# Scores three tiles at a time, statistics turned in the sums' bank, and pieces at new places, in an attention and FFN block

## The chip, the core and the metric

The kernel runs on one core of a Trainium2 chip. The core has a matrix engine (TensorE, PE in the profile; its weight loads are PEld), a vector engine (DVE), a scalar engine for functions such as exp (ACT), a general engine (POOL), and a queue engine that issues most of the DMA transfers (SP). Each engine executes its own instructions in program order and waits for others by semaphores. PE writes its results to PSUM, a memory of eight banks of 512 floats for each of 128 partitions; DVE and ACT read them there, POOL does not.

The metric is the time of one execution on the device, in microseconds (us). Before the change it is 1064.85 us, the median of three runs (1061.61, 1064.85 and 1066.0).

## What is computed

The input `x` is 16 batches of 512 rows of 128 numbers. With `xn`, the normalised rows of `x`, the result is `x + attention(xn) + ffn(xn)`. In short:

```
q, k, v = xn @ Wq, xn @ Wk, xn @ Wv          # 16 heads; 8 numbers a head for q, k; 64 for v
scores  = q . k / sqrt(8), causal
ctx     = softmax(scores) @ v                # per head, over 512 keys
attn    = concat(ctx) @ Wo
xr, xk  = mixes of xn with the row before it, by mu_r and mu_k
ffn     = sigmoid(xr @ W_r.T) * (square(relu(xk @ W_k.T)) @ W_v.T)
out     = x + attn + ffn
```

Everything is float32.

## The kernel before

**Units and slots.** The heads go by pairs: two heads sit in partitions 0 to 63 and 64 to 127 of the same tile, so that PE computes both at once. Two pairs make a group `g`, four groups a batch `b`. The causal half of a group's scores is cut into blocks of 128 rows (or keys), and these are packed into five units, `u` = 0 to 4, each of which fills a PSUM tile of two banks (512 columns for each of the two heads). `ROW_UNITS` and `KEY_UNITS` (lines 31 to 44) list what each unit holds. There are 20 units in a batch and 320 in all. The main loop (line 612) goes through *slots*, one for each unit; a batch is 20 slots.

**Scores are computed twice.** First by rows: `row_scores` writes a tile `sm` with queries along the partitions, and `row_max` lets DVE take the maximum over each row (one instruction for each block and head, `CUSTOM_DVE_ANT` in the profile, followed by a short read of its accumulator). When a group's maxima are complete, `turn_stats` transposes them on PE into a tile `pm`, DVE splits them into a high and a low part (`mh`, `ml`), and SP copies these into rows of `q`, where they take part in the second computation. Then by keys: `key_scores` writes a tile `sT` with keys along the partitions, from which the maximum is already subtracted; ACT takes the exponential (`weights`, tile `e`), POOL zeroes what lies above the diagonal (`mask_weights`) and adds up the blocks of a pair (`add_weights`, tile `acc`). The rows run eight slots (`LEAD`) ahead of the keys.

**From weights to output.** `sum_weights` sums the weights over the keys on PE with a matrix of ones (tile `z`), and ACT takes the logarithm (`half`); `invert_sums` makes reciprocals of it with two more instructions on ACT and copies each to the other heads' partitions by SP (`recip`). Five slots (`LAG`) after the keys, `weigh` multiplies the weights with `v` on PE, into a tile `av` of one bank for each pair; `take_ctx` lets DVE multiply `av` by `recip` into `ctx`. `project_out` multiplies a group's two `ctx` with `Wo` (tile `po`) and DVE adds that to the FFN's result. `store` transposes the sum back (`yT`), DVE adds `x`, and SP stores it.

**Pieces.** The rest is cut into pieces that are placed at slots by the calls of `at` (lines 518 to 553): the eight products of `project_v` (tile `pv`, read by ACT), `project_qk` (tiles `pq` and `pk`; ACT takes the high part, DVE then the low part, SP writes both to DRAM and `spread_qk` brings them back), `transpose_xn`, the three products of the FFN (`ffn_k`, `ffn_r`, `ffn_out`), the moments and the layernorm of a later batch. Each has a slot and a place in it: -1 ahead of the scores, 0 and 1 after them, 2 at the slot's end.

**What sets the order.** `slot_work` (lines 559 to 595) writes the instructions down, and `_InOrder` keeps each engine's own in that order. In each slot: `turn_stats` where due, the pieces of place -1, `row_scores` and `key_scores`, in the slots with `u` = 4 the first pair's sums, then what ACT, POOL and DVE do with the scores, the pieces of places 0 and 1, `weigh`, in the slots with `u` = 1 the second pair's sums, `take_ctx` in those with `u` = 1 (first pair) and `u` = 4 (second pair), and the pieces of place 2.

**PSUM.** All eight banks are in use (lines 95 to 97): three buffers of two banks for the score tiles (`ps_sc`, which also gives the tile `pm`), one bank for `av`, and one bank, `ps_m`, for all other products in turn (`m_tile`: the sums `z`, `pv`, `pq`, `pk`, `po`, the FFN's, the transposes). A tile's next user waits until the last reader of the one before is done.

**Two ways of using PE.** `product`, `weigh` and `sum_weights` use four columns of 32 at a time, with all 128 rows of the array. The scores use 33 or 35 rows and 128 columns, for two heads at a time.

Of the kernel before, what the change touches and what calls it, by code (L numbers as in the profile page):

```python
# [9 lines left out]
FP = mybir.dt.float32  # L10
# [5 lines left out]
P = 128  # L16
# [6 lines left out]
UNITS = 5  # L23
LEAD = 8
LAG = 5
# [37 lines left out]
def attn_ffn_kernel(  # L63
# [19 lines left out]
    N_UNITS = B * PER_BATCH  # L83
# [11 lines left out]
    ps_sc = ctx.enter_context(tc.tile_pool(name="ps_sc", bufs=3, space=PSUM))  # L95
# [14 lines left out]
    def m_tile(name):  # L110
        return ps_m.tile([P, 512], FP, tag="m", name=name)
# [204 lines left out]
    def row_scores(n):  # L316
        b, g, u = place(n)
        q, k = qs[b % 2], ks[b % 2]
        sm = sms[n] = ps_sc.tile([P, 2, 512], FP, tag="sc", name=f"sm_{n}")
        for pair, i, at_col in ROW_UNITS[u]:  # L320
            p = 2 * g + pair
            for h in range(2):
                s = slice(64 * h, 64 * h + RS)
                pe.matmul(
                    sm[:, h, at_col : at_col + (i + 1) * P],
                    q[s, p, i * P : (i + 1) * P], k[s, p, : (i + 1) * P],
                    start=True, stop=True,
                )
# [13 lines left out]
                    accum_out=stats[b, g][:, h, pair, i : i + 1],  # L342
                )

    def turn_stats(b, g):
        mx = stats.pop((b, g))
        pm = ps_sc.tile([P, 2, 512], FP, tag="sc", name=f"pm_{b}_{g}")[:, 0]
        pe.transpose(pm[0 : 4 * NB, 0:P], mx.rearrange("q h p i -> q (h p i)"), ident)
        hi = stat.tile([4 * NB, P], FR, tag="mh", name=f"mh_{b}_{g}")
        lo = stat.tile([4 * NB, P], FR, tag="ml", name=f"ml_{b}_{g}")  # L350
        dve.tensor_copy(hi, pm[0 : 4 * NB, 0:P])
        dve.tensor_tensor(lo, pm[0 : 4 * NB, 0:P], hi.bitcast(FP), ALU.subtract)
        for n, half in enumerate((hi, lo)):
            for h in range(2):
                r = 64 * h + RS + n
                sp.dma_start(
                    out=qs[b % 2].bitcast(FP)[r : r + 1, 2 * g : 2 * g + 2, :].rearrange(
                        "o p (i t) -> o (p i) t", t=P
                    ),
                    in_=half.bitcast(FP)[2 * NB * h : 2 * NB * h + 2 * NB],  # L360
                )
# [5 lines left out]
    def place(n):  # L367
        b, r = divmod(n, PER_BATCH)
        return (b, *divmod(r, UNITS))

    def key_scores(n):
        b, g, u = place(n)
        q, k = qs[b % 2], ks[b % 2]
        st = sts[n] = ps_sc.tile([P, 2, 512], FP, tag="sc", name=f"sT_{n}")
        for pair, j, at_col in KEY_UNITS[u]:
            p, w = 2 * g + pair, T - j * P
            for h in range(2):
                s = slice(64 * h, 64 * h + RA)
                pe.matmul(
                    st[:, h, at_col : at_col + w],  # L380
                    k[s, p, j * P : (j + 1) * P], q[s, p, j * P : T],
                    start=True, stop=True,
                )

    def weights(n):
        e = es[n] = ep.tile([P, 2, 512], FP, tag="e", name=f"e_{n}")
        act.activation(e, sts.pop(n), AF.Exp)

    def mask_weights(n):

        e, parts = es[n], KEY_UNITS[n % UNITS]
        if n % UNITS == 2:
            blocks = [e.rearrange("k h (s q) -> k (h s) q", q=256)[:, :, 0:P]]
        else:
            blocks = [e[:, :, at_col : at_col + P] for _, _, at_col in parts]
        for d in blocks:
            pool.affine_select(
                out=d, in_=d, compare_op=ALU.is_ge, fill=0.0, base=0,
                pattern=[[0, d.shape[1]], [1, P]], channel_multiplier=-1,
            )  # L400
# [29 lines left out]
                acc[:, :, P:256], es[n][:, :, P:256], es[n - 1][:, :, 0:P], ALU.add  # L430
            )

    def sum_weights(q0, pair):


        e0, acc = es[q0 + 4 * pair], accs.pop((q0, pair))
        z = m_tile(f"z_{q0}_{pair}")
        for part in range(2):
            for c in range(2):
                if part and c:  # L440
                    continue
                lo, hi = ((0, P), (256, T))[c] if part == 0 else (P, 256)
                for h in range(2):
                    r = 64 * c + 32 * h
                    pe.matmul(
                        z[r : r + 32, lo - 256 * c : hi - 256 * c], ones[:, 0:32],
                        (acc if lo else e0)[:, h, lo:hi],
                        start=True, stop=True, skip_group_check=True,
                    )
        half = small.tile([P, 256], FP, tag="half", name=f"half_{q0}_{pair}")  # L450
        act.activation(half, z[:, 0:256], AF.Ln)
        recips[q0, pair] = half
# [57 lines left out]

    todo = {}

    def at(slot, where, f, *args):
        todo.setdefault((slot, where), []).append((f, args))

    for b in range(-1, B):
        s0 = b * PER_BATCH
        n = b + 2  # L520
        if n < B:
            first = n == 1
            for c in range(NB):
                at(c - 7 if first else s0 + 1 + c, 0, row_moments, n, c)
            at(-4 if first else s0 + 5, 0, layernorm, n)
            at(-3 if first else s0 + 6, 0, scale_xn, n)
            at(-3 if first else s0 + 8, 2 if first else 1, transpose_xn, n)
            at(-2 if first else s0 + 10, 2 if first else -1, project_qk, n, False)
            at(-1 if first else s0 + 15, 2 if first else -1, project_qk, n, True)
            for i in range(4):  # L530
                at(i if first else s0 + 20 + i, 0, spread_qk, n, False, i)
                at(i + 4 if first else s0 + 24 + i, 0, spread_qk, n, True, i)
        if b + 1 < B:
            places = ((5, -1), (8, 2), (12, 1), (13, 1), (13, 2), (17, 1), (23, 1), (23, 2))
            if b < 0:
                places = ((-8, 1), (-7, 1), (-6, 1), (-5, 1), (-4, 1), (-3, 1), (-1, 1), (3, 1))
            for n, (slot, where) in enumerate(places):
                at(slot + max(s0, 0), where, project_v, b + 1, n)
        if b < 0:
            at(-6, 2, turn_weights)  # L540
            continue
        if b + 3 < B:
            at(s0 + 12, 0, load_x, b + 3)
        at(s0 - 5, 0, mix, b, 1)
        at(s0 - 3, 0, mix, b, 0)
        at(s0 - 2, 1, ffn_k, b)
        at(s0, -1, ffn_r, b)
        at(s0, 0, ffn_log, b)
        at(s0 + 1, 0, ffn_sig, b)
        at(s0 + 2, 1, ffn_out, b)  # L550
        for g in range(NQ):
            at(s0 + 5 * g + 10, 2, project_out, b, g)
        at(s0 + 27, 1, store, b)

    def run(s, where):
        for f, args in todo.pop((s, where), ()):
            f(*args)

    def slot_work(s):
        rows = s + LEAD if s + LEAD < N_UNITS else None  # L560
        keys = s if 0 <= s < N_UNITS else None
        av = s - LAG if 0 <= s - LAG < N_UNITS else None
        u = s % UNITS
        turned = s + LEAD - UNITS
        if turned >= 0 and turned % UNITS == 0 and turned < N_UNITS:
            b, g, _ = place(turned)
            turn_stats(b, g)
        run(s, -1)
        if rows is not None:
            row_scores(rows)  # L570
        if keys is not None:
            key_scores(keys)
        first_sums = u == 4 and 0 <= s - 4 < N_UNITS
        if first_sums:
            sum_weights(s - 4, 0)
        if keys is not None:
            weights(keys)
            mask_weights(keys)
            add_weights(keys)
        if first_sums:  # L580
            invert_sums(s - 4, 0)
        if rows is not None:
            row_max(rows)
        run(s, 0)
        run(s, 1)
        if av is not None:
            weigh(av, only=1 if u == 2 else None)
            if u == 1:
                sum_weights(s - 6, 1)
                invert_sums(s - 6, 1)  # L590
                weigh(av + 1, only=0)
                take_ctx(av - 1, 0)
            if u == 4:
                take_ctx(av - 4, 1)
        run(s, 2)
# [13 lines left out]
    load_weights()  # L609
    for b in range(1, min(B, 3)):  # L610
        load_x(b)
    for s in range(-LEAD, N_UNITS + LAG):
        slot_work(s)
    for s, where in sorted(todo):
        run(s, where)
# [31 lines left out]
```

## Time and profile before

| | |
|---|---|
| median of three runs | 1064.85 us |
| the profiled execution, its own time | 1067.56 us |
| its span in the profile | 1065.8 us |
| PE busy | 965.3 us, 91% of the span |
| DVE busy | 790.7 us, 74% |
| POOL busy | 771.8 us, 72% |
| ACT busy | 669.1 us, 63% |
| chain that ended last: PE, ACT, DVE, POOL | 41%, 24%, 14%, 11% |
| row maxima on DVE: 1024 instructions | 508.4 us, mean 497 ns |
| reads of their accumulators: 1024 | 143.7 us, mean 140 ns |
| exponential of a key tile on ACT: 320 | 326.8 us, mean 1021 ns |
| a copy of `pv` on ACT: 128 | 76.2 us, mean 595 ns |
| logarithm of the sums on ACT: 128 | 49.0 us, mean 383 ns |
| reciprocals on ACT: 256 | 106.3 us, mean 415 ns |
| add of `po` on DVE: 64 | 44.1 us, mean 689 ns |

The span goes from the first instruction to the last of one profiled execution; the execution's own time has what lies around it too. An engine is busy while an instruction of it is under way, whether or not anything depends on it. Matmuls overlap each other, so for PE the distance from one start to the next says more than the length of one. A line of the timeline gives the start and the length in us, the engine, the line of the source, the instruction, what it writes and reads, the shape, how many were merged, and in brackets the idle time before it with what ended that. All kernel instructions carry line 57, that of the helper which records them, so they are told apart by their tiles. The granted clock of TensorE is 1.0 at full speed.

### The profile page before, as it was taken

The page shows a single profiled execution, that of the slowest core. Times are in us where ns is not written, and L with a number is a line of the kernel's source. Part 1 is how long each engine was busy: PE and PEld are TensorE (multiplying, and loading weights), DVE is VectorE, ACT ScalarE, POOL GpSimd, SP SyncE. Part 2 cuts the span into 40 slices and gives each one's busy share as a digit, 9 for nine tenths or more (in the row PEclk, how much of TensorE's full clock was granted, in tenths as well). Part 3 has the DMA queues.
Part 4 walks back from the last instruction along what each step waited for, and adds up shares of the span by engine and source line. Part 5 has one row for each costly group of instructions (what it writes and reads, how often), then busy time and mean ns, then how long its engine had stood idle before and what let it go on. Part 6 is the DMA issues. An engine that isn't in the chain of part 4 may idle for free.

```text
span 1065.8 us, 28371 instructions
## 1 busy us (share of the span) xinstructions
PE 965.3 (91%) x10563; PEld 417.8 (39%) x10563; DVE 790.7 (74%) x2628; ACT 669.1 (63%) x1041; POOL 771.8 (72%) x996
## 2 busy tenths in 40 slices
PE   1679999999999999999999999999999999999996
PEld 0123444344444434444443444344444444444442
DVE  1547787787878778787877788787778878778752
ACT  1235766757576666757676675767667676766752
POOL 3126877877787787878778787877778787778883
PEclk9957999999999999999999999999999999999999
DMA  5644254353626334362544436263443635352011
GB/s 122 107 80 82 52 92 96 62 95 73 102 64 98 89 70 86 72 106 69 91 90 76 78 72 106 69 94 87 76 80 79 98 80 87 72 83 46 20 35 26
DMA packets 61450, 84.25 MB, mean 79 GB/s; under 512 B 12208, under 2 KB 48688, under 8 KB 59264
## 3 DMA queue, kind: packets, MB, share of 16 engines
q1 hardware_dynamic: 58624, 80.79, 41.3%
q8 instruction: 84, 1.38, 0.6%
q0 software_dynamic: 448, 0.26, 0.4%
q10 hardware_dynamic: 2240, 1.38, 0.4%
q14 instruction: 54, 0.44, 0.2%
HBM read 39.13 MB, written 25.17 MB: 60 GB/s over the span
## 4 chain that ended last, share of the span: by engine, by line
PE 41%; ACT 24%; DVE 14%; POOL 11%; issue 6%; DMA 3%; SPq 0%; ACTq 0%; DVEq 0%; POOLq 0%
PE av L57 10%; ACT e L57 9%; PE po L57 8%; POOL acc L57 8%; PE pv L57 6%; PE z L57 5%; DVE sm L57 5%; ACT recip L57 4%; PE sm L57 4%; POOL e L57 3%; ACT e_sig L57 3%; PE sT L57 2%; ACT v L57 2%; PE pk L57 2%; DVE ffn L57 2%
## 5 line engine op out<-in xcount | busy, mean ns | idle before, releaser
L57 DVE CUSTOM_DVE_ANT_0 sm<-sm,row_mask 128x384 f32<-128x384 f32 (+3 forms) x1024 | 508.4, 497 | 136.8 <-PE sm L57 111.5
L57 ACT ACTIVATE e<-sT 128x1024 f32<-128x1024 f32 x320 | 326.8, 1021 | 150.3 <-PE sT L57 140.1
L57 PE MATMUL av<-e,v 128*32 128x512 f32 (+3 forms) x4096 | 353.1, 438 | 2.8 <-DVE ctx L57 2.7
L57 POOL TENSOR_SCALAR_AFFINE_SELECT e<-e 128x256 f32<-128x256 f32 (+1 forms) x448 | 197.0, 454 | 198.1 <-ACT e L57 193.9
L57 POOL TENSOR_TENSOR acc<-acc,e 128x256 f32<-128x256 f32 (+1 forms) x256 | 257.8, 1007 | 15.4
L57 POOL TENSOR_TENSOR acc<-e,e 128x768 f32<-128x768 f32 (+2 forms) x192 | 245.8, 1280 | 0.0
L57 PE MATMUL sm<-k,q 33*128 33x384 f32 (+3 forms) x1024 | 165.1, 379 | 20.1 <-DMA k<-kd 19.2
L57 PEld LDWEIGHTS av<-e,v 128*32 128x32 f32 x4096 | 127.3, 109 | 138.0 <-issue 106.2
L57 PEld LDWEIGHTS sm<-k,q 33*128 33x128 f32 x1024 | 83.5, 189 | 214.9 <-issue 112.2
L57 PE MATMUL pv<-wv,xnT 128*32 128x512 f32 x1024 | 143.3, 631 | 6.0 <-DVE ffn L57 4.4
L57 DVE DVE_READ_ACCUMULATOR2_ANT mx<- 128x1 f32 x1024 | 143.7, 140 | 0.0
L57 PE MATMUL sT<-q,k 35*128 35x384 f32 (+3 forms) x1024 | 137.3, 325 | 1.5 <-DVE mx L57 0.7
L57 ACT ACTIVATE v<-pv 128x512 f32<-128x512 f32 x128 | 76.2, 595 | 86.5 <-PE pv L57 71.8
L57 PE MATMUL po<-ctx,wo 128*32 128x512 f32 x1024 | 122.5, 595 | 7.6 <-DVE ql L57 3.2
L57 ACT ACTIVATE half<-z 128x256 f32<-128x256 f32 x128 | 49.0, 383 | 101.6 <-PE z L57 101.6
L57 DVE TENSOR_TENSOR ctx<-av,recip 128x512 f32<-128x512 f32 x128 | 87.7, 685 | 30.8 <-PE av L57 22.9
L57 ACT ACTIVATE recip<-half 64x256 f32<-64x256 f32 x256 | 106.3, 415 | 6.3
L57 PEld LDWEIGHTS sT<-q,k 35*128 35x128 f32 x1024 | 93.3, 189 | 11.6 <-issue 2.5
L57 PE MATMUL z<-acc,ones 128*32 128x256 f32 (+1 forms) x1024 | 79.4, 331 | 1.8 <-POOL acc L57 1.8
L57 POOL TENSOR_TENSOR xmix<-xmix,prev 128x512 f32<-128x512 f32 x32 | 41.0, 1281 | 43.9 <-ACT prev L57 43.9
L57 PEld LDWEIGHTS po<-ctx,wo 128*32 128x32 f32 x1024 | 30.2, 109 | 93.3 <-issue 47.6
L57 PE MATMUL z<-e,ones 128*32 128x128 f32 x512 | 51.9, 278 | 10.5 <-DVE ffn L57 4.1
(73 smaller groups left out, 632.6 us busy)
## 6 DMA issues: line engine op xcount, KB each, us to landing
recip<-recip SPq DMA_DIRECT2D x256, 64.0 KB
q<-qd SPq DMA_DIRECT2D x60, 256.0 KB
k<-kd SPq DMA_DIRECT2D x60, 256.0 KB
kd<-kh SPq DMA_DIRECT2D x64, 128.0 KB
x<-in_L_attn_x_dram SPq DMA_DIRECT2D x16, 256.0 KB
qd<-qh SPq DMA_DIRECT2D x32, 128.0 KB
qd<-ql SPq DMA_DIRECT2D x32, 128.0 KB
kd<-kl SPq DMA_DIRECT2D x32, 128.0 KB
```

The lines of the kernel that those rows point to most:

```text
L57: return self._tc.keep_in_program_order(f(*args, **kwargs))
```

## The change

The loop of slots is written anew. Scores are no longer computed in each slot, but twice in three slots, three tiles at a time: in slots `s` that are a multiple of 3 a row tile (unit `s + 8`), a key tile (`s`) and a row tile (`s + 9`); in the slot after it, behind the sums and the pieces of place 1, a key tile (`s`), a row tile (`s + 9`) and a key tile (`s + 1`). What ACT, POOL and DVE do with the three tiles follows: first the key tiles', then the row tiles' maxima.

The sums of a group's first pair move from the slot with `u` = 4 to the next one with `u` = 0, those of the second pair from `u` = 1 to `u` = 2. The transposed statistics no longer take a score buffer: `turn_stats` gets the columns 256 to 511 of the same bank of `ps_m` into whose columns 0 to 255 the second pair's sums are then written. The pieces get new places; place -1 is gone, and place 1 lies between the sums and the second stage of scores. The loop begins one slot earlier.

```diff
-    def turn_stats(b, g):
+    def turn_stats(b, g, pm):
         mx = stats.pop((b, g))
-        pm = ps_sc.tile([P, 2, 512], FP, tag="sc", name=f"pm_{b}_{g}")[:, 0]
         pe.transpose(pm[0 : 4 * NB, 0:P], mx.rearrange("q h p i -> q (h p i)"), ident)
...
-    def sum_weights(q0, pair):
+    def sum_weights(q0, pair, z):
         e0, acc = es[q0 + 4 * pair], accs.pop((q0, pair))
-        z = m_tile(f"z_{q0}_{pair}")
...
-            at(-3 if first else s0 + 8, 2 if first else 1, transpose_xn, n)
-            at(-2 if first else s0 + 10, 2 if first else -1, project_qk, n, False)
-            at(-1 if first else s0 + 15, 2 if first else -1, project_qk, n, True)
+            at(-3 if first else s0 + 8, 2, transpose_xn, n)
+            at(-2 if first else s0 + 11, 2 if first else 1, project_qk, n, False)
+            at(-1 if first else s0 + 14, 2 if first else 1, project_qk, n, True)
...
-            places = ((5, -1), (8, 2), (12, 1), (13, 1), (13, 2), (17, 1), (23, 1), (23, 2))
+            places = ((6, 1), (9, 1), (12, 2), (13, 2), (16, 1), (17, 2), (22, 2), (24, 1))
...
-        at(s0 - 2, 1, ffn_k, b)
-        at(s0, -1, ffn_r, b)
-        at(s0, 0, ffn_log, b)
-        at(s0 + 1, 0, ffn_sig, b)
-        at(s0 + 2, 1, ffn_out, b)
+        at(s0 - 1, 1, ffn_k, b)
+        at(s0 + 1, 1, ffn_r, b)
+        at(s0 + 1, 0, ffn_log, b)
+        at(s0 + 2, 0, ffn_sig, b)
+        at(s0 + 3, 2, ffn_out, b)
...
-        at(s0 + 27, 1, store, b)
+        at(s0 + 27, 2, store, b)
...
+    def scores(units):
+        units = [(keys, n) for keys, n in units if 0 <= n < N_UNITS]
+        for keys, n in units:
+            (key_scores if keys else row_scores)(n)
+        for keys, n in units:
+            if keys:
+                weights(n)
+                mask_weights(n)
+                add_weights(n)
+        for keys, n in units:
+            if not keys:
+                row_max(n)
+
+    def sums(s):
+        u = s % UNITS
+        if u == 0 and s >= UNITS:
+            q0, pair = s - UNITS, 0
+        elif u == 2:
+            q0, pair = s - 2 - UNITS, 1
+        else:
+            return
+        summed = 0 <= q0 < N_UNITS
+        turned = u == 2 and 0 <= s + 3 < N_UNITS
+        if summed or turned:
+            z = m_tile(f"z_{s}")
+            if turned:
+                b, g, _ = place(s + 3)
+                turn_stats(b, g, z[:, 256:512])
+            if summed:
+                sum_weights(q0, pair, z)
+                invert_sums(q0, pair)
+
     def slot_work(s):
...
+        if s % 3 == 0:
+            scores(((False, s + LEAD), (True, s), (False, s + LEAD + 1)))
+        sums(s)
+        run(s, 1)
+        if s % 3 == 1:
+            scores(((True, s), (False, s + LEAD + 1), (True, s + 1)))
         run(s, 0)
         if av is not None:
             weigh(av, only=1 if u == 2 else None)
             if u == 1:
-                sum_weights(s - 6, 1)
-                invert_sums(s - 6, 1)
                 weigh(av + 1, only=0)
                 take_ctx(av - 1, 0)
             if u == 4:
                 take_ctx(av - 4, 1)
         run(s, 2)
...
-    for s in range(-LEAD, N_UNITS + LAG):
+    for s in range(-LEAD - 1, N_UNITS + LAG):
```

More of the change, by code (lines that the diff above doesn't have):

```diff
@@ L533, in attn_ffn_kernel @@
         if b + 1 < B:
-            places = ((5, -1), (8, 2), (12, 1), (13, 1), (13, 2), (17, 1), (23, 1), (23, 2))
+            places = ((6, 1), (9, 1), (12, 2), (13, 2), (16, 1), (17, 2), (22, 2), (24, 1))
             if b < 0:
-                places = ((-8, 1), (-7, 1), (-6, 1), (-5, 1), (-4, 1), (-3, 1), (-1, 1), (3, 1))
+                places = ((-9, 1), (-8, 1), (-7, 1), (-6, 1), (-5, 1), (-4, 1), (-1, 1), (3, 1))
             for n, (slot, where) in enumerate(places):
@@ L557, in run @@
             f(*args)
+    def scores(units):
[28 more added lines that the diff above has]
+                invert_sums(q0, pair)
     def slot_work(s):
-        rows = s + LEAD if s + LEAD < N_UNITS else None
-        keys = s if 0 <= s < N_UNITS else None
         av = s - LAG if 0 <= s - LAG < N_UNITS else None
         u = s % UNITS
[L564 to L583, printed above, removed]
+        if s % 3 == 0:
[4 more added lines that the diff above has]
+            scores(((True, s), (False, s + LEAD + 1), (True, s + 1)))
         run(s, 0)
-        run(s, 1)
         if av is not None:
```

## The prediction

> **What bounds the kernel now.** The summary comes first, then one period, then its instructions. (Times in us; columns of the timeline: start, length, engine, instruction.)
>
> ```profile
> PE 965.3 (91%) x10563; PEld 417.8 (39%) x10563; DVE 790.7 (74%) x2628; ACT 669.1 (63%) x1041; POOL 771.8 (72%) x996
> 464.84:526.69 61.85, 58.52 (x663) 25.77 (x661) 49.20 (x165) 41.70 (x66) 47.86 (x62) 1.00 0.46 84
> ```
>
> The second line is one batch (20 slots) by the windows view, PE, PEld, DVE, ACT, POOL, clock. Transposes of the output start 61.85 apart, so a slot takes 61.85/20 = 3.09 and 15 slots 46.4. PE is busy 58.5 of 61.9: it is the bound, but DVE has 49.2 and serves it in strict order, so PE's margin against DVE is small.
>
> ```profile
> 504.36 1.06 PE L57 MATMUL av<-e,v 128*32 128x512 f32 x8
> 505.24 1.90 PE L57 MATMUL po<-ctx,wo 128*32 128x512 f32 x16
> 507.07 0.50 PE L57 MATMUL sm<-k,q 33*128 33x512 f32 x2
> 507.41 0.40 PE L57 MATMUL sT<-q,k 35*128 35x384 f32 x4
> 507.74 1.07 PE L57 MATMUL av<-e,v 128*32 128x384 f32 x16
> ...
> 1032.23 0.49 PE L57 MATMUL sT<-q,k 35*128 35x512 f32 x2
> 1032.65 0.41 PE L57 MATMUL z<-e,ones 128*32 128x128 f32 x4
> ```
>
> Read starts, not lengths, since matmuls overlap. A product of 512 columns costs 0.86 (half of po's 16), so po should take 1.72; it takes 505.24 to 507.07 = 1.83, so a turn to scores costs 0.11. Two score tiles take 507.07 to 507.74 = 0.67; one, in the tail, 1032.23 to 1032.65 = 0.42. A further tile is thus 0.25, and three take 0.92. With 0.03 on the way back (504.36 to 505.24 is 0.88, not 0.86) a stage of two costs 0.81, of three 1.06.
>
> ```profile
> 477.62 0.69 DVE L57 CUSTOM_DVE_ANT_0 sm<-sm,row_mask 128x512 f32<-128x512 f32 x1
> 478.23 0.14 DVE L57 DVE_READ_ACCUMULATOR2_ANT mx<- 128x1 f32 x1
> 478.40 0.70 DVE L57 CUSTOM_DVE_ANT_0 sm<-sm,row_mask 128x512 f32<-128x512 f32 x1
> 479.01 0.14 DVE L57 DVE_READ_ACCUMULATOR2_ANT mx<- 128x1 f32 x1
> 479.55 0.69 DVE L57 TENSOR_TENSOR ctx<-av,recip 128x512 f32<-128x512 f32 x1 [0.39 <-PE av L57]
> 480.16 0.27 DVE L57 CAST mh<-pm 16x128 fp32r<-16x128 f32 x1
> 480.46 0.28 DVE L57 TENSOR_TENSOR ml<-pm,mh 16x128 fp32r<-16x128 f32 x1
> 480.67 0.68 DVE L57 CUSTOM_DVE_ANT_0 sm<-sm,row_mask 128x512 f32<-128x512 f32 x1
> ```
>
> A row tile's maxima cost DVE 2 x 0.78 = 1.56 for the units with one part (u 0 and 4); the same view gives 2.06 to 2.1 for the others. ctx takes 0.61, mh with ml 0.55 until ml is done. In this kernel mh and ml read a score buffer of their own (pm), and no sums wait for them.
>
> **The change, part by part.** PE issues the same instructions in another order, so only turns, waits and places have a price.
>
> Turns. 15 slots had 15 stages of two tiles, 15 x 0.81 = 12.15; now 10 stages of three, 10 x 1.06 = 10.6. Gain 1.55 per 15 slots. The transpose pm stood directly ahead of scores (0.20 to the next start) and now stands ahead of sums; a turn there may cost 0 to 0.31 more (0.11 + 0.17 + 0.03, the part of a one-tile stage above 0.25); I take 0.08, as its own length is 0.28.
>
> Statistics in the sums' bank. In PE's order of the changed kernel each slot with u = 2 has pm, then the sums; its first sum waits for the semaphore count that ml sets. Before, no such wait exists. Queued behind it on PE are the sums, weigh and all later products; for the sums wait ACT's logarithm and reciprocals, SP's two copies of these, and ctx. And ml is in DVE's order behind whatever row maxima stand there: in slots that are a multiple of 3, two whole tiles of them. Sums start 0.03 after ml. Row by row that is the main cost, and the walk below prices it.
> The Trainium skill ("PSUM — Partial Sum Buffer", PSUM bank collisions) says why the wait is there: accesses are to be kept apart by bank and 32-partition quadrant, not by address, so sums in other columns of the bank still have to wait. No run here shows what an unguarded access does; if only addresses counted, the term would be nothing.
>
> Three tiles in three buffers. The third tile of a stage needs the buffer whose maxima come last. Its place is 0.70 into the stage.
>
> One bank for all single products (ps_m). Scores used to lie between po of a u = 0 slot and the next product; in two of three cases they no longer do, and that product waits for DVE's add on po (0.61), itself queued behind maxima. POOL's masks and sums of weights come in pairs now, but what reads them comes three slots later, some 10 us, against 2.4 per slot of POOL work: hidden; without that cover up to one slot's 2.4. SP issues mh's and ml's four copies later in the slot, still two slots or more ahead of the key scores that read them; hidden. The first sums move from u = 4 to the next u = 0, and with them the reciprocals' copies on SP; ctx stays in u = 1, two slots (some 6) later, where the waits view of before has a single wait for such a copy: hidden; if not, DVE's queue stops for what is left of the copy.
>
> **The walk.** 15 slots in five blocks of three; stage 1.06, first tile readable at 0.60, second 0.85; sums 0.43; weigh 0.86 (1.29 in u = 1, 0.43 in u = 2); po 1.72; pieces 0.86; ACT: exp 1.02, logarithm 0.38, two reciprocals 0.85, copy 0.60. Times from each block's start, the commonest piece at each place; A, C are the maxima of the first stage, B of the second.
> Slots 0-2: A, C end 4.26 (ctx until 0.6, 2.1, 1.56). PE: stage, sums, weigh, po to 4.07; add 4.26-4.9; the piece waits 0.85, to 5.78; stage 6.84; weigh 8.13; pm 8.41; B to 8.19, ctx 8.9, ml 9.45; sums wait 1.06, to 9.9; weigh; piece waits 0.14; end 11.33.
> Slots 3-5: A, C to 4.8. Stage, weigh, piece 2.78; its copy 3.55; next piece waits 0.8, to 4.43; stage 5.49; B 5.28-7.38; weigh, sums 6.78; ctx 8.0 frees the av bank: weigh waits 1.24; po; end 10.6.
> Slots 6-8: add 0.77, A, C to 3.89, ctx 4.5, ml 5.05. Stage, piece, weigh, pm 3.5; sums wait 1.57, to 5.5; stage, weigh, piece, weigh 8.71; ACT's copy is behind two exps, 9.5: 0.8; end 10.38.
> Slots 9-11: A, C 4.8, ctx 5.41. Stage, piece, weigh, sums 3.21; third tile waits 0.91, weigh for ctx 0.25, po 8.0, add 8.8, piece waits 0.8, weigh; end 10.95.
> Slots 12-14: ctx 0.76, A, C 4.42, ml 4.97. Stage, pm 1.34; sums wait 3.66; weigh, piece (0.14) 6.86; stage, weigh, piece 9.64; copy behind two exps, 0.77; piece, weigh; end 12.14.
> Sum 55.4, of it 13.0 waits. Other pieces at these places (k's low half, the FFN product, none) move the blocks by +0.35, -0.5, +0.4 and -0.4: 55.2, against 46.4. That is +8.8 in 15 slots. Some 300 slots run so (the first few are load-bound, the last eight have no rows): 20 x 8.8 = 176. DVE's small pieces, left out so far, are per batch four moments (0.29), layernorm 1.2, scaling 0.7, the sigmoid's 0.69: 3.75; half of them fall where DVE is late: 1.9 x 15 = 28. So 1065.8 + 176 + 28 = 1270. The profiled execution took 1067.6 by its own time, its span 1065.8, the median run 1064.9; the difference of 1 is below what the sum can say, and 1270 stands for both.
>
> **The clock.** A wait of 3.66 is longer than any at full clock in the steady part. The profile shows what waits can do:
>
> ```profile
> 50.00:60.00 10.00, 7.10 (x38) 1.85 (x36) 5.07 (x17) 3.41 (x6) 3.28 (x4) 0.71 0.02 3
> 60.00:70.00 10.00, 7.26 (x32) 1.67 (x32) 3.64 (x13) 1.92 (x4) 0.00 (x0) 0.50 0.53 117
> 70.00:80.00 10.00, 6.05 (x33) 2.85 (x35) 7.25 (x23) 5.45 (x8) 5.59 (x7) 0.50 0.55 94
> 90.00:95.00 5.00, 4.46 (x57) 2.08 (x55) 3.95 (x11) 3.26 (x5) 4.25 (x5) 0.83 0.66 82
> ```
>
> The granted clock (third from last) fell to 0.5 about 54, after a wait of 1.61, and came back about 92, after 15 of dense matmuls from 76 on; in the tail waits of 0.9 to 1.35 left it at 1.0. If every 3.66 takes it down, the 6.2 of PE work behind it in that block takes 12.4 in place of 7.1 with its waits: 5.3, 20 times, 106. From both sides: 0 to 106; I take 0 in the likeliest case, since one event is little to go by.
> The Trainium skill ("TensorE: Matmul & The Clock Gate", Part 1) puts the fall at an idle window of about 3.4: by that 3.66 is just enough only in a lucky phase, so its sum is nearer 1270; the profile's fall after 1.61 speaks against so high a limit.
>
> **The rivals.**
> (1) The clock falls: 1270 + 106 = 1376. For it, the rows above; against it, the tail.
> (2) Only the wait for ml counts, 1.06 + 1.57 + 3.66 = 6.29 in 15 slots less the 1.55 gained, the other waits being no more than before's: 20 x 4.74 = 95, so 1161. For it, DVE idles 111 for scores now and would catch up; against it, the product after po has nothing between.
> (3) Faster: the waits vanish behind other work, 1065.8 - 20 x 1.55 = 1035. One mechanism decides: the gain of 1.55 holds if ml is done about when the sums are due; DVE's 74% speaks for room, its order against. It turns where each of the three turned statistics in 15 slots waits 1.55/3 = 0.52.
> (4) The stages don't come as told. PE's order shows three tiles at a time throughout, so this has nothing for it; 1066.
>
> **How the numbers follow.** Likeliest, 1220 to 1320: 0.46. Clock, above 1320: 0.25. Part, 1075 to 1220: 0.19. Faster, 0.08; the fourth, 0.02. Range 1165 to 1390: it leaves out the faster cases, the lower part of (2), and a clock down for longer. Faster or slower is meant beyond 0.5%, what this measurement can tell: 0.08, 0.02, 0.90.
>
> **What would show it.** Right: DVE's ml as releaser of the first sum, some 60 times, about 2.1 each (130 in all), 3 to 4 in every third; PE below 80% busy; a batch of about 74; products released by DVE's add; score stages of 0.92 + turn. Wrong: sums that start within 0.3 of pm, DVE's maxima back to back with PE still dense, or a batch under 62. A clock row below 1.0 in the middle is rival (1).

## The result, and the profile after

The changed kernel took 1446.19 us, the median of four runs (1444.08 to 1447.3); the kernel before, beside it on the same chip, 1064.68. The ratio is 1.359, with a 95% interval of 1.355 to 1.362. The prediction was 1270, with a range of 1165 to 1390: the direction was right, and the time lies above the range. The profiled execution has a span of 1444.1 us, 378 more than before.

First the page's busy times and its row of granted clock, and the mean clock of the core before (the first of the two lines of that view) and after:

```profile
PE 1093.0 (76%) x10563; PEld 470.9 (33%) x10563; DVE 801.0 (55%) x2628; ACT 671.7 (47%) x1041; POOL 770.6 (53%) x996
...
PEclk7579889978898997889799888989997899899989
```

```profile
core 0: 1065.8 us, clock 0.982
```

```profile
core 0: 1444.1 us, clock 0.859
```

The counts of instructions are those of before, and so are the busy times of DVE, ACT and POOL. PE's share fell from 91% to 76% although its busy time rose by 128 us, for the same matmuls: they ran longer. The clock row says why. Where nearly every slice before had a 9, there are now 7s and 8s over the whole length. As the clock in this trace stands at 1.0 or 0.5, a mean of 0.859 is half speed for 2 x (1 - 0.859) = 28% of the span, some 407 us; before, 0.982 gives 38 us, most of it at the start. The records of the clock begin at 14.9 us in this trace and only at 50.7 in that of before; what PE does ahead of them is at half clock too (a product's eight matmuls take 1.93 to 1.94 there, 1.07 at full clock), and the mean leaves it out.

A batch is no longer one repeating period: the transposes of the output start 82.8, 94.1 and 85.8 us apart, again and again, since the pattern of stages repeats after 15 slots and the batch after 20, together after 60. The next line is the windows view over three batches (columns as in the prediction's batch line: window, length, PE, PEld, DVE, ACT, POOL, clock, DMA share, GB/s).

```profile
527.30:790.20 262.90, 203.62 (x1981) 88.51 (x1981) 149.75 (x492) 125.61 (x196) 143.22 (x184) 0.86 0.31 59
```

That is 87.6 a batch where it was 61.85. DVE has 49.9 of work in each, 49.2 before, so no engine has become the bound: all of them wait for one another. What PE waits for, from the waits view (total, times, longest):

```profile
PE z L57 <- DVE ml L57: 174.8, 62, 5.6
PE pv L57 <- DVE ffn L57: 36.0, 30, 2.4
PE av L57 <- DVE ctx L57: 19.5, 27, 1.6
...
PE sT L57 <- DVE mx L57: 16.8, 18, 1.5
```

The first line is the wait that the prediction named, 62 times as told, but with a mean of 2.82 where 2.1 was said. The others are the ones of the walk: products behind DVE's add on `po`, `weigh` behind `ctx`, the third tile of a stage behind the maxima.

One of these waits, in a slot that is a multiple of 3, seen first on PE and then on DVE (start, length, engine, instruction, and in brackets the idle time before it and who ended it):

```profile
636.78 0.50 PE L57 MATMUL sm<-k,q 33*128 33x512 f32 x2
637.12 0.40 PE L57 MATMUL sT<-q,k 35*128 35x256 f32 x4
637.36 0.40 PE L57 MATMUL sm<-k,q 33*128 33x384 f32 x4
637.69 0.28 PE L57 MATMUL z<-ident,mx 128*16 128x128 f32 x1
641.62 0.43 PE L57 MATMUL z<-e,ones 128*32 128x128 f32 x2 [3.65 <-DVE ml L57]
...
643.29 1.97 PE L57 MATMUL pv<-wv,xnT 128*32 128x512 f32 x8
645.19 0.80 PE L57 MATMUL sT<-q,k 35*128 35x384 f32 x4
```

```profile
637.53 0.69 DVE L57 CUSTOM_DVE_ANT_0 sm<-sm,row_mask 128x512 f32<-128x512 f32 x1
...
640.89 0.27 DVE L57 CAST mh<-z 16x128 fp32r<-16x128 f32 x1
641.19 0.28 DVE L57 TENSOR_TENSOR ml<-z,mh 16x128 fp32r<-16x128 f32 x1
```

PE writes the transposed statistics into the bank at 637.69, and the sums could follow. DVE has just begun the maxima of the two row tiles and comes to `mh` only at 640.89; the sums start at 641.62. Then look at the product `pv`: from 643.29 to the next start at 645.19 it takes 1.90, where a product of 512 columns takes 0.86 at full clock. The windows over that place show it (the third figure from the end is the clock):

```profile
634.50:637.90 3.40, 3.40 (x43) 1.69 (x43) 1.64 (x3) 0.87 (x2) 1.20 (x2) 1.00 0.16 36
637.90:641.30 3.40, 0.06 (x1) 0.00 (x0) 3.23 (x14) 0.75 (x1) 1.90 (x2) 0.75 0.54 121
641.30:644.70 3.40, 3.08 (x28) 1.39 (x28) 0.17 (x1) 1.21 (x3) 0.00 (x0) 0.50 0.05 11
644.70:648.10 3.40, 3.40 (x38) 1.88 (x34) 1.47 (x6) 2.54 (x3) 0.92 (x3) 0.75 0.16 40
648.10:651.50 3.40, 2.68 (x28) 0.73 (x22) 0.90 (x3) 1.19 (x2) 3.32 (x4) 1.00 0.00 0
```

The wait empties the second window, and half way through it the clock falls to 0.5, for 6.8 us. So the wait is paid twice: 3.65 us of nothing, and then work at half speed.

**Where the 378 us are.** PE's time is split in three, from the trace. Its idle time rose from 100.5 to 351.1 (+251). In the stretches at half clock, those ahead of the clock's first record included, it was busy 347 us (50 before); half of that is what the clock added: 174 less 25, +148 before rounding. What is left of busy time, as if at full clock, fell from 940 to 920 (-21). 251 + 148 - 21 = 378. The split rests on modelled lengths of overlapping matmuls, so the last term is rough. It counts PE's time and doesn't say by itself what caused which.

### The profile page after: what moved, and what is told of

The parts are those of the page before. It is cut to its first block, busy times and chain, and to the rows that moved or that the text cites. A ratio compares the mean times of both kernels' runs of the same rounds, so it can differ in the third digit from the quotient of the medians.

```text
span 1444.1 us, 28393 instructions
## 1 busy us (share of the span) xinstructions
PE 1093.0 (76%) x10563; PEld 470.9 (33%) x10563; DVE 801.0 (55%) x2628; ACT 671.7 (47%) x1041; POOL 770.6 (53%) x996
## 4 chain that ended last, share of the span: by engine, by line
PE 52%; DVE 28%; ACT 8%; issue 5%; POOL 3%; DMA 3%; SPq 0%; DVEq 0%; ACTq 0%; POOLq 0%
PE av L57 15%; DVE sm L57 15%; PE pv L57 9%; PE po L57 6%; PE sT L57 5%; PE sm L57 5%; PE z L57 4%; DVE ctx L57 4%; DVE mx L57 3%; DVE ffn L57 2%; ACT e_sig L57 2%; POOL acc L57 2%; ACT e L57 2%; DMA qd<-qh 2%; PE pk L57 2%
## 5 line engine op out<-in xcount | busy, mean ns | idle before, releaser
L57 PE MATMUL av<-e,v 128*32 128x512 f32 (+3 forms) x4096 | 389.9, 492 | 19.9 <-DVE ctx L57 19.5
L57 ACT ACTIVATE e<-sT 128x1024 f32<-128x1024 f32 x320 | 317.6, 1023 | 153.4 <-PE sT L57 150.3
L57 PE MATMUL pv<-wv,xnT 128*32 128x512 f32 x1024 | 170.4, 742 | 50.1 <-DVE ffn L57 36.0
L57 PE MATMUL z<-e,ones 128*32 128x128 f32 x512 | 60.5, 316 | 185.0 <-DVE ml L57 174.8
L57 PE MATMUL sT<-q,k 35*128 35x384 f32 (+3 forms) x1024 | 167.7, 388 | 17.5 <-DVE mx L57 16.8
L57 PEld LDWEIGHTS sT<-q,k 35*128 35x128 f32 x1024 | 104.3, 222 | 106.2 <-issue 72.3
L57 PEld LDWEIGHTS sm<-k,q 33*128 33x128 f32 x1024 | 99.8, 218 | 108.4 <-issue 94.3
L57 PEld LDWEIGHTS z<-e,ones 128*32 128x32 f32 x512 | 24.8, 117 | 235.7 <-issue 128.3
L57 DVE TENSOR_TENSOR ffn<-po,ffn 128x512 f32<-128x512 f32 x64 | 44.2, 691 | 96.8 <-PE po L57 96.6
L57 PE MATMUL z<-acc,ones 128*32 128x128 f32 (+1 forms) x1024 | 95.8, 385 | 0.2 <-POOL acc L57 0.2
```

The source lines that it names most:

```text
L57: return self._tc.keep_in_program_order(f(*args, **kwargs))
```

## The experiments

Each kernel is compared with the kernel before, run on the same chip beside it (1067.8 to 1068.6 us).

### The bank that the statistics share with the sums

**`own_buffer`**: the changed kernel, with `pm` again in a score buffer.

```diff
-    def turn_stats(b, g, pm):
+    def turn_stats(b, g):
         mx = stats.pop((b, g))
+        pm = ps_sc.tile([P, 2, 512], FP, tag="sc", name=f"pm_{b}_{g}")[:, 0]
...
```

> The changed kernel, but the transposed statistics take a score buffer again, as before the change. Theory A (the wait of the sums for ml, and the falls of the clock that follow it): the 174.8 us of waits for ml go, and with them most of the falls, so half-speed time falls from 411 us to under 150; the third score tile may wait up to 1 us for its buffer at each of 62 turns. 1140 to 1230 us. Theory B (three score tiles in three buffers are what costs, the bank is innocent): the waits come back at the score tiles, PE stays under 80% busy, above 1380 us.

1281.2 us, ratio 1.200 (1.193 to 1.207): some 165 below the changed kernel, and still 213 above the one before. The waits view shows that no sum waits for `ml` any more, and what stands in its place:

```profile
PE av L57 <- DVE ctx L57: 45.9, 43, 3.0
PE pv L57 <- DVE ffn L57: 33.2, 30, 2.4
PE pm L57 <- ACT e L57: 21.2, 20, 1.4
PE sT L57 <- ACT e L57: 21.1, 12, 2.2
```

The wait for `ctx` more than doubled, and now `pm` takes a score buffer and waits for the exponential to free it. The mean clock is 0.924. So the bank costs some 165 here, less than half of the 378, and the stages and places the other 213. By the same split, what goes with the bank is 97 us of idle time and 90 of half clock, with 21 more of work. The result lies between the two theories.

**`bank_alone`**: the kernel before, with the statistics turned in the bank of the second pair's sums, both in the slots with `u` = 2; stages of two tiles and all pieces as before.

```diff
+        if u == 2:
...
+                z = m_tile(f"z_{s}")
+                if turned:
+                    b, g, _ = place(s + 3)
+                    turn_stats(b, g, z[:, 256:512])
+                if summed:
+                    sum_weights(s - 7, 1, z)
+                    invert_sums(s - 7, 1)
...
```

> The kernel before, with its stage of two score tiles in each slot and its places, but with the statistics turned in the bank of the second pair's sums, both at the start of the slot with u = 2. Theory A: the wait for ml is set by what DVE has queued; here that is what is left of one row tile and one ctx. From before's trace ml ended 1.05 us after pm, so 62 x 1.05 = 65 us, and waits that short leave the clock up: about 1130 us. Theory D (the shared bank costs the same wherever it stands): 62 x 2.8 = 175 us and falls of the clock: 1240 us or more.

1172.9 us, ratio 1.099 (1.096 to 1.101), +105.

```profile
PE z L57 <- DVE ml L57: 60.8, 60, 1.4
PE pk L57 <- ACT v L57: 24.3, 16, 1.6
...
PE z L57 <- DVE mx L57: 17.7, 49, 3.2
PE z L57 <- DVE st L57: 16.9, 13, 1.3
```

With one row tile at a time ahead of it on DVE, `ml` is 1.0 late and not 2.8: much the same edit (here it also moves the second pair's sums a slot later) costs 105 in one order and 165 in the other. The transposes wait too (`mx`, `st`), as this place is earlier than they can be served. Here the clock stayed at 1.0 nearly throughout: after the start-up there was one fall, at 990 us, and one in the last 6 us.

**`turn_first`**: in the slots that are a multiple of 3, the turn and the sums ahead of the first stage, so that DVE has not yet the two row tiles in front of `ml`.

```diff
+        sums(s)
         if s % 3 == 0:
             scores(((False, s + LEAD), (True, s), (False, s + LEAD + 1)))
-        sums(s)
```

> The changed kernel, but in slots that are a multiple of 3 the statistics and sums come ahead of the first stage of scores, so that ml no longer stands behind two tiles of row maxima in DVE's order. Theory A: the 20 waits of 3.7 to 5.6 us (4.3 on average) shrink to about 1 us, 66 us less, and the falls after them go, some 4 us each, 80 us less: about 1300 us. Theory B: DVE is late anyway and the time moves to the next wait: above 1400 us.

1379.5 us, ratio 1.292 (1.290 to 1.295): 67 less than the changed kernel, and near neither number. The `ml` waits fell from 174.8 to 119.8, and the waits of score tiles for maxima rose from 16.8 to 28.9: DVE's work that no longer stands ahead of `ml` stands ahead of the next thing. By the split, 30 of the 67 are idle time and 47 half clock, with 12 more of work.

**`sums_first`**: the sums first, and the statistics turned into the bank behind them.

```diff
-            if turned:
-                b, g, _ = place(s + 3)
-                turn_stats(b, g, z[:, 256:512])
             if summed:
                 sum_weights(q0, pair, z)
                 invert_sums(q0, pair)
+            if turned:
+                b, g, _ = place(s + 3)
+                turn_stats(b, g, z[:, 256:512])
```

> The changed kernel, but in slots with u = 2 the sums come ahead of the turned statistics in the shared bank. Now pm waits for ACT's logarithm of the sums (0.4 us or more), and what waits for ml is the next product that needs the bank, behind 0.43 us of weigh. Theory A (the bank makes PE wait for DVE's queue wherever ml stands): the waits move from the sums to that product and stay long, 110 us or more in all, and the clock still falls: 1380 to 1440 us. Theory H (only the sums' wait matters): 1270 to 1300 us, as with a buffer of their own.

1334.3 us, ratio 1.252 (1.243 to 1.260): 112 less, between the theories.

```profile
PE z L57 <- ACT half L57: 48.2, 62, 2.0
PE pv L57 <- DVE ml L57: 38.3, 26, 3.2
```

Two users of one bank wait for each other in either order. Now the transpose waits for ACT's logarithm, 0.78 each time, and the next product, which needs the bank, for `ml`; but ACT is less late than DVE, and a wait that is split in two is less often long: PE has 18 waits of 2.4 or more after the first 100 us, where the changed kernel has 42.

### The clock

**`fill_wait`**: the changed kernel, with four products more between `pm` and the sums in the slots that are a multiple of 3, 4 x 0.86 = 3.44 us of work for PE. They write into the `av` bank that is used next, and `weigh` overwrites them.

```diff
+FILL = 4
...
+            if summed and turned and s % 3 == 0:
+                av = avs[q0, 1] = ps_av.tile([P, T], FP, tag="av", name=f"av_{q0}_1")
+                for i in range(FILL):
+                    product(av, wo[:, i % NPAIR, :], wv[:, 0:512])
```

> The changed kernel with 3.4 us of extra products on PE between the turned statistics and the sums in slots that are a multiple of 3, written into the bank of the next av tile and overwritten by it; nothing else changes. PE has 20 x 3.4 = 69 us more to do, all of it inside the waits of 3.7 to 5.6 us. Theory A with the clock: no fall after these waits, half-speed time down by about 20 x 6.8 = 136 us, the time down by 50 to 90 us, to 1355 to 1395. Theory C (the clock is a by-product, the waits alone count): 1446 us or a little more.

1374.4 us, ratio 1.286 (1.284 to 1.289): 72 us less than the changed kernel, with more work. A slot of the same kind as above, PE and then windows:

```profile
666.50 0.28 PE L58 MATMUL z<-ident,mx 128*16 128x128 f32 x1
667.13 3.64 PE L58 MATMUL av<-wv,wo 128*32 128x512 f32 x32 [0.36 <-DVE ctx L58]
671.08 0.30 PE L58 MATMUL z<-e,ones 128*32 128x128 f32 x2 [0.31 <-DVE ml L58]
```

```profile
666.40:669.80 3.40, 3.04 (x33) 0.96 (x33) 3.30 (x11) 1.02 (x1) 1.91 (x2) 1.00 0.01 2
669.80:673.20 3.40, 3.01 (x42) 1.48 (x34) 1.33 (x7) 1.21 (x3) 0.00 (x0) 1.00 0.02 5
673.20:676.60 3.40, 2.71 (x38) 1.34 (x38) 2.39 (x9) 2.54 (x3) 2.00 (x3) 1.00 0.20 45
```

The sums come no earlier, 4.58 after the transpose (3.93 above), but PE is not idle, and the clock stays at 1.0 behind it. 672 matmuls were added, 21 times 3.44 = 72 us. Split as above: idle time 351 to 277 (-74), what half clock added 174 to 92 (-82), the work at full clock +84; sum -72. So the filled waits were replaced by work of about their own length, and the gain is the clock's. That the waits take the clock down, and that this costs time by itself, is shown.

### The stages of three tiles and the places

**`stages_alone`**: the kernel before, with the stages of three alone; sums, bank and pieces as before, and the loop begun one slot earlier with one start-up piece moved with it.

```diff
-        if rows is not None:
-            row_scores(rows)
-        if keys is not None:
-            key_scores(keys)
+        if s % 3 == 0:
+            scores(((False, s + LEAD), (True, s), (False, s + LEAD + 1)))
+        if s % 3 == 1:
+            scores(((True, s), (False, s + LEAD + 1), (True, s + 1)))
...
```

> The kernel before with one part of the change: scores in stages of three tiles, twice in three slots; its sums, its pieces (but the very first product of v) and its statistics in a score buffer stay as before. Theory A: a stage of three needs all three score buffers and gives DVE two row tiles at once (4 us), so ctx, the third tile and the next product wait; what own_buffer still has above before (213 us) is mostly this: 1130 to 1230 us. Theory E (stages of three are worth their saved turns, about 31 us, and the rest comes from places and sums): 1030 to 1060 us.

1215.2 us, ratio 1.138 (1.136 to 1.141), +147; the theory in which the stages by themselves lose holds.

```profile
PE sT L57 <- DVE mx L57: 36.8, 55, 1.5
...
PE av L57 <- DVE ctx L57: 14.1, 16, 2.0
PE z L57 <- DVE ffn L57: 13.3, 14, 1.3
...
PE sm L57 <- ACT e L57: 10.6, 9, 1.2
```

A stage of three needs all three score buffers within a microsecond, so it waits for the last of the readers; none of these waits is long, but they come close together, and the mean clock is 0.925. By the split, 94 of the 148 us between the two spans are idle time and 49 half clock. The clock fell 18 times after the first 100 us, though no wait of PE there is longer than 2.1.

**`maxima_late`**: `stages_alone`, with the maxima of the second row tile of a stage put at the slot's end, behind DVE's add and `ctx`.

```diff
-        for keys, n in units:
-            if not keys:
-                row_max(n)
+        rows = [n for keys, n in units if not keys]
+        for n in rows[:1]:
+            row_max(n)
+        return rows[1:]
...
+        for n in late:
+            row_max(n)
```

> stages_alone, but in slots that are a multiple of 3 DVE takes the second row tile's maxima at the slot's end, behind ctx and the pieces. Theory K (what stages of three cost is DVE's order: ctx, ml and the add on po stand behind two tiles of maxima): 1150 to 1190 us. Theory L (it is the buffers: the third tile of the next stage waits for those maxima, and they are only later now): 1215 us or more.

1217.6 us, ratio 1.142 (1.137 to 1.148): no gain over `stages_alone`. The buffer came free later instead: score tiles waited 44.3 for maxima (36.8), and row tiles 38.7 for the exponential's buffer (10.6). Another order on DVE doesn't make room where all buffers are wanted at once.

**`two_tiles`**: `own_buffer` with a stage of two tiles in each slot, so that of the change only the new places of the pieces and of the sums are left.

```diff
-        if s % 3 == 0:
-            scores(((False, s + LEAD), (True, s), (False, s + LEAD + 1)))
+        scores(((False, s + LEAD), (True, s)))
...
-        if s % 3 == 1:
-            scores(((True, s), (False, s + LEAD + 1), (True, s + 1)))
```

> own_buffer (the changed kernel with its statistics in a score buffer) but with a stage of two tiles in each slot, as before: the new places and the moved sums without stages of three. Theory A: near before, 1060 to 1100 us, full clock. Theory E (the places and the moved sums cost): above 1150 us.

1146.0 us, ratio 1.074 (1.069 to 1.080), +78, which neither theory had. A line of PE's waits, and one of DVE's:

```profile
PE av L57 <- DVE ctx L57: 62.3, 48, 3.0
```

```profile
DVE ctx L57 <- DMA recip<-recip: 43.8, 30, 5.3
```

With the sums moved to `u` = 0 and `ctx` still in `u` = 1, the copies of the reciprocals are no longer done when DVE wants them. In the changed kernel that wait is small (13.7, 3 times) and in `own_buffer` in between (27.2, 9 times), in the order of the lengths of their slots. The two edits together give 147 + 78 = 225, near the 213 of `own_buffer`, which has both.

**`sums_back`**: `two_tiles` with the sums where they were before (`u` = 4 and `u` = 1), to see whether they make the 78.

```diff
-        if u == 0 and s >= UNITS:
-            q0, pair = s - UNITS, 0
-        elif u == 2:
-            q0, pair = s - 2 - UNITS, 1
-        else:
+        q0, pair = s - 4, 0
+        if u not in (2, 4):
             return
...
                 weigh(av + 1, only=0)
+                sum_weights(s - 6, 1, m_tile(f"z_{s}"))
+                invert_sums(s - 6, 1)
```

> two_tiles with the sums back where they were before the change (the first pair's in u = 4, the second's in u = 1); stages of two tiles, statistics in a score buffer, only the pieces at their new places. In two_tiles weigh waits 62 us for ctx, and ctx for the reciprocals' copies. Theory I (the moved sums make ctx late): those waits go, 1065 to 1090 us. Theory J (the pieces' places cost): 1130 us or more.

1163.9 us, ratio 1.092 (1.085 to 1.099): 18 more, not less: theory I's time didn't come.

```profile
PE av L57 <- DVE ctx L57: 35.0, 35, 1.7
PE pk L57 <- ACT half L57: 22.0, 29, 0.8
PE pv L57 <- ACT half L57: 19.1, 30, 0.9
```

The waits for `ctx` were nearly halved, from 62.3 to 35.0, and 41 us of new ones came: a piece of place 1 now lies directly behind the sums in the one bank and waits for ACT's logarithm. Pieces and sums fit each other; how the 78 divide between them stays open.

**`cover_po`**: `own_buffer`, with the pieces of the slots with `u` = 1 put behind `weigh`, to cover the wait for the add on `po`.

```diff
-        run(s, 1)
+        if u != 1:
+            run(s, 1)
...
+        if u == 1:
+            run(s, 1)
+            run(s, 0)
```

> own_buffer, but in slots with u = 1 the piece comes after weigh, so that 1.29 us of PE work lie between po and the product that needs its bank. Theory A: the waits of such products for DVE's add (54 us in own_buffer) mostly go, with the falls of the clock that follow those of 2.4 us: 1210 to 1240 us. Theory G (DVE is the bound, and its time comes back at the next wait): above 1265 us.

1299.0 us, ratio 1.216 (1.211 to 1.220), 18 more than `own_buffer`. The wait aimed at did go, from 33.2 to 14.6, and others took its place: `pm` and the key tiles behind the exponential from 42.3 to 55.3, and sums behind a copy of `pv` (11.4) and row tiles behind maxima (11.2) came into the list.

### A version that beats both

**`mix_late`**: the kernel before, with one call put later in its slot. `mix` has two instructions on ACT (0.72 each for `xmix`), which stood ahead of a copy of `pv` that the next product waits for.

```diff
-        at(s0 - 3, 0, mix, b, 0)
+        at(s0 - 3, 2, mix, b, 0)
```

> The kernel before, with the FFN's second mix moved to the end of its slot, so that ACT copies v before it mixes and not after. In before's trace pk waits 0.95 us for that copy in 16 slots, 15 us in all. If that wait is on the path: 1048 to 1055 us, 1% below before; if the time comes back at the next wait: 1062 to 1068 us.

1050.6 us (1050.2 to 1053.1), ratio 0.985 (0.983 to 0.987), as expected: a gain of 1.5%, small but clear of the interval. One wait on PE, first in the kernel before, then here:

```profile
PE pk L57 <- ACT v L57: 15.2, 16, 1.0
```

```profile
PE pk L57 <- ACT v L57: 0.7, 1, 0.7
```

## Why the prediction was wrong in its size

Set against the split of the 378 us, the prediction's own terms (waits: 176 + 28, plus the 31 of the turns' gain that is inside the 176):

| | predicted | measured |
|---|---|---|
| turns saved, 20 x 1.55; measured: the rest of the split | -31 | -21 |
| PE's waits | +235 | +251 |
| clock | 0 (bounds 0 to 106) | +148 |
| sum | +204 | +378 |

**The step that failed is the clock.** The working had the row that speaks for it (the fall after a wait of 1.61 at the start), priced it at 106 at most, and then took 0, "since one event is little to go by"; it measured 148. (The longest wait of the tail that spoke against it is 1.18 in the trace, not 1.35.) It was an error of choice and of size. Of choice, since the clock fell 51 times. Of size, since only the wait of 3.66 was priced, 20 times: 43 of the 51 falls come within 4.5 us of a PE wait of 2.4 or more, of all three places of the turn and of the products behind DVE's add, and most last 6.8 us. `fill_wait` shows that this is cause and effect for the longest of them. The range's upper end, 1390, held 1376 for that rival and nothing beyond, so it couldn't hold 1446. Rival (1) had the right mechanism; with 148 in place of 106 it gives 1418. A count of long waits isn't enough either: `stages_alone` has 18 falls without a wait above 2.1.

The Trainium skill ("TensorE: Matmul & The Clock Gate", Part 1) gives an idle window of about 3.4 us, free-running. By that rule the prediction leaned towards 0. This trace's falls last 3.41 us or a multiple of it (but for the one at the end), 6.83 most often, and all its changes of the clock lie on one grid of 3.41 us, which agrees with the window; but waits of 2.43, 2.54 and 2.70 took the clock down too, so a wait need not fill a window.

**The wait for `ml`: mechanism right, size too small.** It came 62 times, and takes PE's time as told; 174.8 us against about 130. By place: slots that are a multiple of 3, 4.14 on average (3.66 predicted); the slots after them 2.19 (1.57); the third ones 2.09 (1.06). The term that was too small is DVE's small pieces, and above all the FFN's sigmoid: the working priced it at 0.69 of work for DVE, "half of them fall where DVE is late". At its new place it stands in the slot ahead of a turn in every batch, and DVE, in strict order, waits there for three functions on ACT before it can go on to `ctx` and `ml`. PE's and DVE's timelines at such a place:

```profile
853.77 0.28 PE L57 MATMUL z<-ident,mx 128*16 128x128 f32 x1
858.20 0.42 PE L57 MATMUL z<-e,ones 128*32 128x128 f32 x2 [4.15 <-DVE ml L57]
```

```profile
855.91 1.03 DVE L57 SCALAR_TENSOR_TENSOR sig<-sig,e_sig 128x512 f32<-128x512 f32 x1 [2.01 <-ACT e_sig L57]
856.87 0.68 DVE L57 TENSOR_TENSOR ctx<-av,recip 128x512 f32<-128x512 f32 x1
...
857.77 0.28 DVE L57 TENSOR_TENSOR ml<-z,mh 16x128 fp32r<-16x128 f32 x1
```

Not a row of maxima stands in this wait; DVE itself is idle for 1.9 of it. The 15 turns behind a sigmoid waited 3.5, 5.6 and 4.2 us by place, and that is 35 of the 45 us that the `ml` waits have above 130. At the other places they are 3.7, 1.8 and 1.4 on average, near the walk. The other waits came as walked: 20 x 13.0 - 130 = 130 there, some 124 in the waits view outside the start-up (36.0 + 19.5 + 16.8 + eight smaller lines, 51.5). So the sum of all waits, 235 against 251, was close; in part by luck, as the 28 set aside for DVE's small pieces took up much of the 45.

**The bank.** That the sums wait though their columns are others than the statistics', as the trace of before didn't show, is confirmed by `own_buffer` and `sums_first`: the wait goes with the shared bank, and turns round with the order.

**The turns** came about as told, where starts can be read: at full clock and without a wait, a stage of three takes 0.96 on average (0.92 predicted), a stage of two in the trace of before 0.69 (0.67), and a product ahead of either 0.99, of which 0.86 is its own. With 10 stages in place of 15 that saves some 1.4 in 15 slots, 28 us in all, near 31. The rest of the split is too rough to say as much: it is -21 here, and 0 in `own_buffer` and +5 in `stages_alone`, which have the same stages.

**What was called hidden.** POOL's masks and the late copies of `mh` and `ml` cost nothing that the waits show. The reciprocals' copies are nearly hidden in the changed kernel, whose slots take 4.4 us (87.6 / 20); in `two_tiles`, at 3.6 us (1146 / 320), they are not. The reason given, a single wait in the trace of before, spoke of another place in the order.

**What the parts cost.** Not separated in the prediction, and now measured: places and sums 78, stages of three 147, the two together 213; the shared bank 165 on top of that. The stages were to gain 31 and their waits were known to the walk; that they lose by themselves is shown by `stages_alone`. Rival (2), that only the `ml` wait counts, is refuted by `own_buffer`, which has none of it and takes 1281. The batch of about 74 was 83 to 94; PE below 80% and the products released by DVE's add were as told.

## What to carry to other kernels

On an engine in strict order, ask of each new wait not only how long it is but what it does to the clock behind it: where the trace shows a single fall after a wait, price every wait of that size in the steady part, and short ones that come close together, and let the range reach to their sum. Sharing a bank joins the queues of all engines that read it, so its price is whatever stands ahead of the reader on its own engine at that moment, small pieces included, with what these wait for themselves. Where all buffers are in use and engines serve each other in order, a wait that is taken away in one place is mostly found again in the next: move one thing that stands ahead of a reader, as `mix_late` does, rather than a whole order.

## What the hardware showed that was not expected

A single idle stretch of TensorE of 2.4 to 2.7 us in an otherwise dense run brought the clock to half, for 3.4 or 6.8 us; behind longer ones it was up to 13.7. Waits of 1.25 to 1.74 in the steady part didn't: the one of 1.25 at 660.1 left the clock at 1.0. Two of 1.0 and 0.9 close together did, four times (at 281, 544, 807 and 1070 us).

The place of a wait decides too. Two waits of the same length, 2.21, begin at 1327.8 and at 1391.3, both at full clock. These are the windows that lie on the grid of the clock's changes around them:

```profile
1325.65:1329.07 3.42, 2.15 (x31) 0.89 (x27) 3.35 (x10) 1.02 (x1) 2.10 (x3) 1.00 0.00 0
1329.07:1332.48 3.41, 2.46 (x40) 1.69 (x44) 1.74 (x7) 1.66 (x4) 1.17 (x2) 1.00 0.04 8
1390.51:1393.92 3.41, 1.20 (x29) 0.56 (x17) 2.81 (x9) 0.00 (x0) 3.26 (x4) 1.00 0.00 0
1393.92:1397.33 3.41, 3.41 (x31) 2.06 (x23) 1.61 (x7) 2.87 (x5) 0.56 (x1) 0.50 0.08 15
```

The first wait is shared between two windows, PE is busy 2.15 and 2.46 in them, and the clock stays. The second falls into one, which leaves PE 1.20, and the clock is at half in the next. Between 100 and 1360 us, all 45 falls of this trace follow a window in which PE was busy for 0.54 of it or less, and the 230 windows that left the clock up have 0.54 or more. This is no rule for other kernels: in `own_buffer` a window with 0.41 left the clock up, and in `stages_alone` one with 0.77 was followed by a fall.

More work made the kernel faster: 72 us of matmuls for nothing in the idle stretches took 72 us off the time.
